# Storing the transposed h and the base by block, and another order of loads, at the border to a recurrence

## The chip, the cores and the metric

The kernel runs on one core of one Trainium2 chip. The metric is the device time of one execution in microseconds; the time before is the median of three runs. The core has a matrix engine (PE, with its weight loads PEld), a vector engine (DVE), a scalar engine (ACT), a general engine (POOL) and a sequencer (SP) that issues most DMAs; POOL issues the others from its own queue. Sixteen DMA engines carry them out.

## The reference: four graph layers, of which the third is a recurrence

For 16 graphs (B) of 1024 nodes (N) with 256 features (D), each layer adds to x a graph operation of h = relu(layernorm(x)). Layers 0 and 1 are products of the adjacency with a linear map of h; layer 3 is an aggregation with a two-layer network. Layer 2 goes through the nodes one after the other:

```python
def step(h, i):
    x = jnp.take(h_e, i, axis=1)
    row = jnp.take(norm_adjT, i, axis=1)
    x_par = jnp.einsum('bj,bjd->bd', row, h)
    iou = x @ W_ioux.T + b_ioux + x_par @ W_iouh.T + b_iouh
    r, z = jnp.split(iou, 2, axis=1)
    r, z = (jax.nn.sigmoid(r), jax.nn.sigmoid(z))
    hc = jnp.tanh(x @ W_coux.T + b_coux + x_par * r @ W_couh.T + b_couh)
    h_new = z * x_par + (1.0 - z) * hc
    h = jax.lax.dynamic_update_slice(h, h_new[:, None, :], (0, i, 0))
    return (h, None)
h_out, _ = jax.lax.scan(step, h_e, jnp.arange(n))
```

## The kernel before

Layers 0 and 1 run together in `layers_0_1`, one graph i per iteration and 16 in all. The order of the work on each engine is written out by hand; a list of hooks puts DVE, ACT, POOL and SP work between the large matmuls (L387, L423). The nodes of each graph are split into 8 blocks (NT) of 128 (P).

Layer 2 does 8 blocks (t), and in each block 8 sub-steps (s) of 16 nodes. All 16 graphs go together: a sub-step has 256 columns, 16 graphs by 16 places. Inside a block the nodes are taken in another order, found at run time and different for each graph; the tables `place` and `table` hold it. A sub-step needs: the gates' part from x (class `Gates`: a POOL copy of 16 columns of each graph from the tile `he` into `hs`, L1039, then three gates of four matmuls each, L1048); the sum over earlier nodes outside the block, `bxt` (made by `base_tasks`, L935 and L949, during the block before; for block 0 loaded from `base_d`); the adjacency inside the block (class `Sub`: POOL gathers its rows from `near_d` into `aj`, L1013, and makes `bd` and `ai` from it, L1029 and L1020); and the weights `wh` (L1102).

What layer 2 needs of h and of the adjacency is made ahead, in a `Job` for each graph, while layer 1 runs. Jobs 0 to 12 run in the iterations i = 9 to 15, two per iteration (an even job, `run_a`, after the first sums, and an odd one, `run_b`, after the second). Jobs 13 to 15 (`tail`) stand behind the last iteration, L814 to L842. Of a job, in its order of work:

- `load` (L511 to L516): SP loads the adjacency pieces `ad` (1 MB) and `ab` (0.5 MB), and h;
- `mask`, `scale`: POOL masks `ad` and `ab` (L524, L526) and scales `ad` (L531, L532); DVE makes `to`, the order as a matrix of ones (L521);
- `turn`: PE transposes h (L542), ACT or DVE copies it to `hT` (L545, L547), POOL stores it (L548);
- `first`: eight matmuls (L554) for the base of block 0, scaled by ACT (L556);
- `order`: PE brings `ad` into the new order (L565, L567), ACT and DVE copy the result to `ao` (L572, L574) after POOL has cleared a corner of it (L561), and POOL stores `near_d` and `next_d` (L575, L576);
- `base`: PE turns the base (L582), DVE copies it (L584), POOL stores it in `base_d` (L585).

`hT` and `ao` of a job share one buffer (both have the name "hT" in a pool with one buffer each), so `ao` is written only when the store of `hT` has read it. The tail jobs use other names: hT of job 14 is in `q`, and so is ao of job 15; ao of job 14 is in `hT`, hT of job 15 in `h1`.

The stores of a job are DMAs on POOL's queue, in this form:

```python
heT_d = dram.tile([B, P, DC, N], F32, name="heT_d")
base_d = dram.tile([B, P, DC, P], F32, name="base_d")
nc.gpsimd.dma_start(heT_d[b], hT)
```

`heT_d` is written in 128 rows of 8 KB for a graph. `load_he(t)` (L998) reads the 128 columns of block t for all graphs, in pieces of 512 bytes: two DMAs of 1 MB (one for each half c of the features), or for block 0 six, since the graphs 0 to 13, 14 and 15 are loaded apart. `bxt` of block 0 is loaded from `base_d` in the same way (L1208).

At the border SP issues in this order: ad and ab of job 14; x; h of graph 15 (a store, L831, that waits for ACT); ad and ab of job 15; wx; four loads of biases; he (six); bxt (six); wh; ab and h for the base of block 1, graphs 0 and 1; he of block 1. POOL's order: the stores and products of jobs 13 to 15, hs for s = 0, the gather aj, bd, ai, hs for s = 1. PE's order: the tail jobs, the gates of s = 0, three matmuls that open the accumulators (L1215), two gates of s = 1, then L1102, the first matmul of the recurrence proper.

Of the kernel before, what the change touches and what calls it, by code (L numbers as in the profile page):

```python
# [9 lines left out]
F32 = mybir.dt.float32  # L10
# [6 lines left out]
P = 128  # L17
B, N, D, H = 16, 1024, 256, 1024
NT = N // P
DC = D // P  # L20
# [22 lines left out]
def gnn_stack(ctx: ExitStack, tc: tile.TileContext, a: dict, out: bass.AP):  # L43
    nc = tc.nc
    const = ctx.enter_context(tc.tile_pool(name="const", bufs=1))
    dram = ctx.enter_context(tc.tile_pool(name="dram", bufs=1, space=DRAM))
# [7 lines left out]

    x2_d = dram.tile([B, N, D], F32, name="x2_d")
    he_d = dram.tile([B, N, D], F32, name="he_d")
    heT_d = dram.tile([B, P, DC, N], F32, name="heT_d")
    hn_d = dram.tile([B, N, D], F32, name="hn_d")
    t_d = {name: dram.tile([B, P, 4, 512], F32, name=name + "_d") for name in ("t1", "t2", "t3", "t4")}

# [10 lines left out]
    table = [const.tile([P, G2, NT, NS], mybir.dt.int32, name=f"table{k}") for k in range(2)]  # L71
    place = const.tile([P, NT * B], F32, name="place")
    dinv = const.tile([P, B, NT], F32, name="dinv")

    def rows(ap):
        return ap.rearrange("(t p) d -> p t d", p=P)
# [9 lines left out]
        nc.gpsimd.tensor_tensor(r, t, mhalf.to_broadcast(shape), ALU.pow)  # L86
        return r

    base_d = dram.tile([B, P, DC, P], F32, name="base_d")
    more = [const.tile([1, N // S], mybir.dt.int32, name=f"more{k}") for k in range(2)]  # L90


# [171 lines left out]
    def layers_0_1():  # L264
        with ExitStack() as st:
            ET = mybir.EngineType
            st.enter_context(tc.manual_schedule(engines={ET.PE, ET.DVE, ET.Activation, ET.Pool, ET.SP}))
            wp = st.enter_context(tc.tile_pool(name="w01", bufs=1))
            big = st.enter_context(tc.tile_pool(name="big01", bufs=1))
# [3 lines left out]
            x, q, h1, h2, g, dis, mean, rs_of, ags = {}, {}, {}, {}, {}, {}, {}, {}, {}  # L273
# [218 lines left out]
            class Job:  # L492
# [42 lines left out]
                def turn(self):  # L535
                    b, to = self.b, self.to
                    hT = big.tile([P, DC, N], F32, name=self.names.get("hT", "hT"))
                    for c in range(DC):
                        for t0 in range(0, NT, 4):
                            pt = psum.tile([P, 512], F32, name="pt")  # L540
                            for t in range(4):
                                nc.tensor.transpose(pt[:, t * P : (t + 1) * P], h2[b][:, t0 + t, c * P : (c + 1) * P],  # L542
                                                    to[:, t0 + t])
                            if t0 == 0 or not self.tail:
                                nc.scalar.copy(hT[:, c, t0 * P : (t0 + 4) * P], pt)  # L545
                            else:
                                nc.vector.tensor_copy(hT[:, c, t0 * P : (t0 + 4) * P], pt)  # L547
                    nc.gpsimd.dma_start(heT_d[b], hT)  # L548

                def first(self):  # L550
                    b = self.b
# [26 lines left out]
                def base(self):  # L578
                    b = self.b
                    pt = psum.tile([P, 512], F32, name="pt")  # L580
                    for c in range(DC):
                        nc.tensor.transpose(pt[:, c * P : (c + 1) * P], self.bs[:, c * P : (c + 1) * P], self.to[:, 0])  # L582
                    bo = self.row("bo").rearrange("p (c i) -> p c i", c=DC)
                    nc.vector.tensor_copy(bo, pt[:, :D].rearrange("p (c i) -> p c i", c=DC))  # L584
                    nc.gpsimd.dma_start(base_d[b], bo)  # L585

                def rest(self):
                    self.first()
# [7 lines left out]
            def side(us):  # L596
                while later:
                    later.popleft()()
                left[0] += us * 1.25
                while left[0] > 0:  # L600
                    cost = next(math, None)
                    if cost is None:
                        break
                    left[0] -= cost
                left[0] = min(left[0], 0.0)
# [37 lines left out]
            job14 = Job(14, {"ad": "at7", "ab": "ds", "to": "at0", "hT": "q", "ao": "hT", "bs": "s1", "bo": "s2"})  # L643
            job15 = Job(15, {"hT": "h1", "ao": "q"})

            for i in range(B):
# [162 lines left out]
                if ahead:  # L809
                    left_of, first, second = combos(q[i + 1])  # L810
                    first()
                side(5.0 if run_a else 3.0)
            h2[14] = big.tile([P, NT, D], F32, name="h2", bufs=2)
            normed(h2[14], x[14], m2.shift, m2.rs, all_)  # L814
            nc.sync.dma_start(rows(he_d[14]), h2[14])
# [9 lines left out]
            job14.mask()  # L825
            run_b.order()
            run_b.base()
            job14.scale()
            h2[15] = big.tile([P, NT, D], F32, name="h2", bufs=2)
            normed(h2[15], x[15], shift, m2.rs, all_)  # L830
            nc.sync.dma_start(rows(he_d[15]), h2[15])  # L831
            job15.load()
            job14.first()
            job14.turn()
            job14.base()
# [3 lines left out]
            job15.base()  # L839
            job15.scale()  # L840
            job14.order()
            job15.order()  # L842
            for _ in math:
                while later:
                    later.popleft()()
# [13 lines left out]
    def layer_2(shared, early):  # L859
        with ExitStack() as st:  # L860
# [5 lines left out]
            def load_w(t, io, co):  # L866
                nc.sync.dma_start(t[:, :, : 2 * D], a[io].rearrange("(c p) e -> p c e", p=P))
                nc.sync.dma_start(t[:, :, 2 * D :], a[co].rearrange("(c p) e -> p c e", p=P))
            load_w(wx, "W_iouxT", "W_couxT")

            bias = wp.tile([P, 3, DC], F32, name="bias")
            bias2 = wp.tile([P, 3, DC], F32, name="bias2")
            with nc.allow_non_contiguous_dma(reason="biases, once"):
                for t, io, co in ((bias, "b_ioux", "b_coux"), (bias2, "b_iouh", "b_couh")):
                    nc.sync.dma_start(t[:, :2].rearrange("p q c -> p (q c)"), a[io].rearrange("(k p) -> p k", p=P))
                    nc.sync.dma_start(t[:, 2], a[co].rearrange("(c p) -> p c", p=P))
            nc.vector.tensor_add(bias, bias, bias2)

            own = wp.tile([P, GB], F32, name="own")
            nc.vector.tensor_reduce(own, ident.rearrange("p (b j) -> p b j", b=GB), AX.X, ALU.add)  # L880
# [14 lines left out]
            def base_tasks(t, bxt):  # L895
# [4 lines left out]
                def load(b):  # L900
                    ab = big.tile([P, NT, P], F32, name="ab")
                    nc.sync.dma_start(ab, a["columns"][b, t])
                    hb = shared.tile([P, NT, D], F32, name="hb")
                    if t > 2:
                        nc.sync.dma_start(hb[:, : t - 2], rows(hn_d[b])[:, : t - 2])
                    if t > 1:
                        nc.sync.dma_start(hb[:, t - 2], hs_d[t - 2][b // GB][b % GB * P : (b % GB + 1) * P])
                    nc.sync.dma_start(hb[:, t:], rows(he_d[b])[:, t:])
                    loaded[b] = ab, hb
# [15 lines left out]
                def task(b, k, held):  # L925
                    def run():
                        if k == 0:
                            if b == 0:
                                mask(0)
                            if b + 1 < B:  # L930
                                load(b + 1)
                            held.append(psum.tile([P, D], F32, name="pf", bufs=3))
                        pb = held[0]
                        ab, hb = loaded[b]
                        nc.tensor.matmul(pb, ab[:, jts[k]], hb[:, jts[k]], start=k == 0, stop=k == len(jts) - 1)  # L935
                        if k == len(jts) - 3 and b + 1 < B:
                            mask(b + 1)
                        if k == len(jts) - 1:
                            del loaded[b]
                            return lambda: summed(b, pb)  # L940
                    return 0.43, run
# [9 lines left out]
                    return 0.44, run  # L951

                load(0)
                tasks = deque()
                for b in range(B):
                    held = []
# [36 lines left out]

            def load_he(t):
                he = big.tile([P, DC, B, P], F32, name="he")
                for b0, b1 in parts if t == 0 else ((0, B),):
                    for c in range(DC):
                        nc.sync.dma_start(he[:, c, b0:b1], heT_d[b0:b1, :, c, t * P : (t + 1) * P].rearrange("b p i -> p b i"))  # L998
                return he

            def row(k, g, t, s):
# [197 lines left out]
                evict()  # L1199

            with tc.manual_schedule(engines={mybir.EngineType.PE, mybir.EngineType.DVE, mybir.EngineType.Activation, mybir.EngineType.Pool}):
                he = load_he(0)
                gx = Gates(he, 0)
                sub = Sub(0, 0)
                bxt = shared.tile([P, DC, B, P], F32, name="bxt")
                for b0, b1 in parts:
                    for c in range(DC):
                        nc.sync.dma_start(bxt[:, c, b0:b1], base_d[b0:b1, :, c].rearrange("b p i -> p b i"))  # L1208
                load_w(wh, "W_iouhT", "W_couhT")
                for task in gx.tasks:  # L1210
                    task()()
                sub.behind()
# [3 lines left out]
                gx.seed_r()  # L1216
                gx.seed_zc()

                near = gx_ahead = None
                behind = []  # L1220
                for t in range(NT):
                    if t == NT - 1:
                        eye = next(early)
                    base_todo = deque()
                    if t + 1 < NT:
                        bxt_next = shared.tile([P, DC, B, P], F32, name="bxt")
                        base_todo = base_tasks(t + 1, bxt_next)
                    n_more = [nc.values_load_multi_w_load_instructions(
# [569 lines left out]
```

## Time and profile before

| | us |
|---|---|
| median of three runs (4225.37 to 4234.3) | 4227.49 |
| the profiled execution | 4226.12 |
| its span, first to last instruction | 4224.4 |
| layer 1 with jobs: 690 to 1297, PE busy | 560.12 of 607 |
| border: 1297 to 1384, PE busy | 58.05 of 87 |
| recurrence after its first sub-step: 1384 to 2960, PE busy | 1525.94 of 1576 |

Times in the profile count from the first instruction. A line of the timeline gives start, duration, engine, line of the kernel, operation, out<-in, shapes and count; in brackets stands how long the engine was idle before, and what ended the wait. POOL's DMA lines are issues: the transfer itself goes on afterwards. SP's issues are marked SPq; where the queue is full, an issue lasts longer. PEclk is the granted share of PE's full clock.

DMA lines of the page:

```profile
DMA  7576657988768454645464554421633434334320
...
q1 hardware_dynamic: 370976, 613.49, 42.5%
q0 software_dynamic: 26080, 109.21, 9.0%
```

q1 is SP's queue, q0 POOL's; the columns are packets, MB and the share of the sixteen engines' time.

### The profile page before, as it was taken

The numbers are of one execution on the slowest core, as the hardware profiler recorded it, in microseconds if no ns is written. First come the engines' busy times: TensorE is split into PE (matmuls) and PEld (weight loads), VectorE is DVE, ScalarE is ACT, GpSimd is POOL, SyncE is SP. The second block draws the span as 40 slices with busy tenths as digits, with TensorE's granted clock in tenths as the row PEclk, the third lists the DMA queues.
The fourth block names the chain that finished last, engine by engine and source line by source line (L and its number), as shares of the span: only waits on it lengthen the run. The fifth ranks groups of instructions, "written<-read, shape, count | busy, mean of one in ns | idle before, by whom it ended". The sixth has DMA issues, their size and how long they took to land. (4 is left out here: it accounts for less than half of the span.)

```text
span 4224.4 us, 56649 instructions
## 1 busy us (share of the span) xinstructions
PE 4018.3 (95%) x19307; PEld 2802.1 (66%) x19307; DVE 2614.6 (62%) x6218; ACT 1635.4 (39%) x4172; POOL 1646.5 (39%) x1740
## 2 busy tenths in 40 slices
PE   7999999998997999999999999998899999999998
PEld 3545455555555888888888888877365665756656
DVE  7888976577762444444444444453577877777776
ACT  3565565544543232232323232323233334333332
POOL 2232223434334324333333333332546355464552
PEclk9999999999998999999999999998899999999999
DMA  7576657988768454645464554421633434334320
GB/s 244 207 238 232 230 200 261 265 301 285 262 212 269 135 197 135 200 136 186 153 193 145 189 163 162 155 99 36 214 120 137 163 120 146 134 121 174 114 100 21
DMA packets 406704, 744.74 MB, mean 176 GB/s; under 512 B 75168, under 2 KB 325664, under 8 KB 365344
## 3 DMA queue, kind: packets, MB, share of 16 engines
q1 hardware_dynamic: 370976, 613.49, 42.5%
q0 software_dynamic: 26080, 109.21, 9.0%
q10 hardware_dynamic: 9216, 16.78, 1.1%
q8 instruction: 210, 3.44, 0.3%
q14 instruction: 222, 1.82, 0.1%
HBM read 538.85 MB, written 183.76 MB: 171 GB/s over the span
## 5 line engine op out<-in xcount | busy, mean ns | idle before, releaser
L86 POOL TENSOR_TENSOR rs<-rs_v,mhalf 128x8 f32<-128x8 f32 (+1 forms) x65 | 112.3, 1728 | 900.4 <-DVE rs_v L82 469.7
L935 PE MATMUL pf<-hb,ab 128*128 128x256 f32 x1568 | 415.2, 383 | 0.0
L1048 PE MATMUL pf<-hs,wx 128*128 128x256 f32 x1536 | 347.7, 383 | 13.0 <-POOL hs L1039 12.7
L1048 PEld LDWEIGHTS pf<-hs,wx 128*128 128x128 f32 x1536 | 293.5, 192 | 56.2 <-POOL hs L1039 13.8
L1348 POOL DMA_INDIRECT hs_d<-h,table x128 | 129.3, 1010 | 464.6 <-ACT gates L1056 404.3
L1576 POOL TENSOR_TENSOR ss<-ss,sq 128x512 f32<-128x512 f32 x224 | 299.2, 1351 | 23.8 <-ACT sq L1574 17.8
L935 PEld LDWEIGHTS pf<-hb,ab 128*128 128x128 f32 x1568 | 272.1, 191 | 37.3 <-issue 6.7
L1053 DVE TENSOR_TENSOR gates<-pf,bias 128x512 f32<-128x512 f32 x128 | 88.5, 692 | 288.3 <-PE pf L1048 248.4
L423 PE MATMUL pmm<-w,ag 128*128 128x256 f32 x1024 | 234.6, 387 | 20.4 <-DVE x L427 8.8
L1639 PEld LDWEIGHTS po<-w,hh 128*128 128x128 f32 x2048 | 237.9, 193 | 16.6 <-issue 11.0
L1639 PE MATMUL po<-w,hh 128*128 128x128 f32 x2048 | 242.1, 277 | 1.4 <-ACT hh L1622 0.7
L423 PEld LDWEIGHTS pmm<-w,ag 128*128 128x128 f32 x1024 | 196.1, 194 | 61.6 <-DVE x L427 12.6
L1574 ACT ACTIVATE sq<-hh 128x512 f32<-128x512 f32 x224 | 141.6, 632 | 197.7 <-POOL ss L1576 118.7
L1522 PE MATMUL ph<-bxt,hb 128*128 128x512 f32 x440 | 198.9, 598 | 4.1 <-ACT hb L1494 2.6
L1146 ACT ACTIVATE r<-pr 128x128 f32<-128x128 f32 (+2 forms) x256 | 57.9, 278 | 366.4 <-PE pr L1102 306.4
L1084 PE MATMUL pf<-bd,h 128*128 128x384 f32 (+4 forms) x512 | 185.1, 451 | 0.8 <-DVE bxt L1087 0.8
L1087 DVE TENSOR_TENSOR bxt<-bxt,pf 128x384 f32<-128x384 f32 (+4 forms) x256 | 128.0, 501 | 82.3 <-PE pf L1084 79.5
L1572 DVE SCALAR_TENSOR_TENSOR hh<-ph,b,u 128x512 f32<-128x512 f32 x192 | 141.5, 749 | 47.0 <-PE ph L1568 36.9
L1622 ACT ACTIVATE hh<-hh,rw 128x512 f32<-128x512 f32 x256 | 158.9, 711 | 24.1 <-DVE hh L1621 24.1
L345 ACT ACTIVATE pt<-x,m_neg 128x256 f32<-128x256 f32 x240 | 114.5, 477 | 109.0 <-DVE m_neg L340 102.7
L1621 DVE TENSOR_TENSOR hh<-hh,po 128x512 f32<-128x512 f32 x256 | 154.3, 679 | 2.9 <-PE po L1618 2.9
L1494 ACT ACTIVATE hb<-x,shift,rs 128x256 f32<-128x256 f32 x120 | 60.9, 591 | 239.6 <-DVE shift L1492 239.6
(371 smaller groups left out, 9283.3 us busy)
## 6 DMA issues: line engine op xcount, KB each, us to landing
at<-in_quarters SPq DMA_DIRECT2D x94, 1024.0 KB
t_d<-at SPq DMA_DIRECT2D x64, 1024.0 KB
ab<-in_columns SPq DMA_DIRECT2D x127, 512.0 KB
bxt<-t_d SPq DMA_DIRECT2D x42, 1024.0 KB
bxt<-in_quarters SPq DMA_DIRECT2D x34, 1024.0 KB
at<-at POOLq DMA_DIRECT2D x30, 1024.0 KB, 7.1
at<-t_d SPq DMA_DIRECT2D x22, 1024.0 KB
pc<-in_own ACTq DMA_DIRECT2D x64, 256.0 KB
```

What stands on the lines that cost most here:

```text
L423: nc.tensor.matmul(po[:, t - t0], ag[:, c, t * P : (t + 1) * P], w[:, c], start=c == 0, stop=c == DC - 1)
L935: nc.tensor.matmul(pb, ab[:, jts[k]], hb[:, jts[k]], start=k == 0, stop=k == len(jts) - 1)
L1048: nc.tensor.matmul(pg[:, e], wx[:, c, q * D + e * P : q * D + (e + 1) * P], self.hs[:, c], start=c == 0, stop=c == DC - 1)
L1084: nc.tensor.matmul(pf, h[:, g, c * P : (c + 1) * P], bd[:, g, b0 : b0 + n, S : S + far], start=True, stop=True)
L1348: nc.gpsimd.indirect_dma_start(out=hs_d[t][g][:, :], out_offset=row(1, g, t, s), in_=h[:, g], in_offset=None)
L1522: nc.tensor.matmul(pa, st[left][:, k], at[q % 6][:, k], start=onto is None and k == 0, stop=k == 3, skip_group_check=True)
L1572: behind3[:] = [nc.vector.scalar_tensor_tensor(hh[q][:, k], ph, b1[:, k : k + 1], u, op0=ALU.add, op1=ALU.add)]
L1574: nc.scalar.activation(sq, hh[q][:, k], AF.Square)
L1576: nc.gpsimd.tensor_tensor(ss[q], ss[q], sq, ALU.add)
L1621: nc.vector.tensor_mul(hh[q][:, k], hh[q][:, k], pr)
L1622: nc.scalar.activation(hh[q][:, k], hh[q][:, k], AF.Silu, scale=rw[:, k : k + 1])
L1639: nc.tensor.matmul(po[:, n], left[:, c, n * P : (n + 1) * P], right[:, c], start=onto is None and n == 0 and c == 0, stop=c == HH - 1, ski ...
```

## The change

1. `heT_d` and `base_d` get another layout: the partition first, then block, half, graph, place. `heT_d[:, t]` is then one run of 16 KB in each partition, and one DMA loads he of a block.
2. A job stores hT in three DMAs: the columns of block 0 at once, the other seven blocks in one DMA for each half (`keep_hT`). Jobs 0 to 12 do all three in `turn`; the tail jobs do the last two after `order` (job 13: after its base).
3. he and bxt of block 0 are loaded in three DMAs each, in turn (graphs 0 to 13, 14, 15).
4. The biases move from the border to the end of iteration 3, their sum to iteration 5, and their tiles to another pool.
5. Job 15's load stands ahead of the store of h of graph 15 on SP; wh is loaded directly behind wx.
6. The gates' inputs for s = 1 are copied directly behind those for s = 0, ahead of the gather aj; the tasks for the base of block 1, with their first two loads, are made ahead of the gates' matmuls.

The order of the instructions on PE and ACT is the same as before; on DVE only the sum of the biases moves.

```diff
-    heT_d = dram.tile([B, P, DC, N], F32, name="heT_d")
+    heT_d = dram.tile([P, NT, DC, B, P], F32, name="heT_d")
+    bias, bias2 = (const.tile([P, 3, DC], F32, name=name) for name in ("bias", "bias2"))
-    base_d = dram.tile([B, P, DC, P], F32, name="base_d")
+    base_d = dram.tile([P, DC, B, P], F32, name="base_d")
...
-                    nc.gpsimd.dma_start(heT_d[b], hT)
+                    nc.gpsimd.dma_start(heT_d[:, 0, :, b], hT[:, :, :P])
+                    self.hT = hT
+                    if not self.tail:
+                        self.keep_hT()
+
+                def keep_hT(self):
+                    for c in range(DC):
+                        nc.gpsimd.dma_start(heT_d[:, 1:, c, self.b], self.hT[:, c, P:].rearrange("p (t i) -> p t i", i=P))
...
-                    nc.gpsimd.dma_start(base_d[b], bo)
+                    nc.gpsimd.dma_start(base_d[:, :, b], bo)
...
+                if i == 3:
+                    with nc.allow_non_contiguous_dma(reason="biases, once"):
+                        for to, io, co in ((bias, "b_ioux", "b_coux"), (bias2, "b_iouh", "b_couh")):
+                            nc.sync.dma_start(to[:, :2].rearrange("p q c -> p (q c)"), a[io].rearrange("(k p) -> p k", p=P))
+                            nc.sync.dma_start(to[:, 2], a[co].rearrange("(c p) -> p c", p=P))
+                if i == 5:
+                    nc.vector.tensor_add(bias, bias, bias2)
...
             run_b.base()
+            run_b.keep_hT()
             job14.scale()
+            job15.load()
             h2[15] = big.tile([P, NT, D], F32, name="h2", bufs=2)
             normed(h2[15], x[15], shift, m2.rs, all_)
             nc.sync.dma_start(rows(he_d[15]), h2[15])
-            job15.load()
...
             job14.order()
+            job14.keep_hT()
             job15.order()
+            job15.keep_hT()
...
             load_w(wx, "W_iouxT", "W_couxT")
-            bias = wp.tile([P, 3, DC], F32, name="bias")
-            bias2 = wp.tile([P, 3, DC], F32, name="bias2")
...
-            nc.vector.tensor_add(bias, bias, bias2)
+            load_w(wh, "W_iouhT", "W_couhT")
...
-                            if b + 1 < B:
+                            if 0 < b < B - 1:
                                 load(b + 1)
...
                 load(0)
+                load(1)
...
                 he = big.tile([P, DC, B, P], F32, name="he")
-                for b0, b1 in parts if t == 0 else ((0, B),):
-                    for c in range(DC):
-                        nc.sync.dma_start(he[:, c, b0:b1], heT_d[b0:b1, :, c, t * P : (t + 1) * P].rearrange("b p i -> p b i"))
+                nc.sync.dma_start(he, heT_d[:, t])
...
-                he = load_he(0)
-                gx = Gates(he, 0)
+                he = big.tile([P, DC, B, P], F32, name="he")
+                bxt, bxt_next = (shared.tile([P, DC, B, P], F32, name="bxt") for _ in range(2))
+                for b0, b1 in parts:
+                    nc.sync.dma_start(he[:, :, b0:b1], heT_d[:, 0, :, b0:b1])
+                    nc.sync.dma_start(bxt[:, :, b0:b1], base_d[:, :, b0:b1])
+                gx, gx_ahead = Gates(he, 0), Gates(he, 1)
                 sub = Sub(0, 0)
-                bxt = shared.tile([P, DC, B, P], F32, name="bxt")
-                for b0, b1 in parts:
-                    for c in range(DC):
-                        nc.sync.dma_start(bxt[:, c, b0:b1], base_d[b0:b1, :, c].rearrange("b p i -> p b i"))
-                load_w(wh, "W_iouhT", "W_couhT")
+                base_todo = base_tasks(1, bxt_next)
...
-                near = gx_ahead = None
+                near = None
```

More of the change, by code (lines that the diff above doesn't have):

```diff
@@ L869, in layer_2 @@
             load_w(wx, "W_iouxT", "W_couxT")
-            bias = wp.tile([P, 3, DC], F32, name="bias")
-            bias2 = wp.tile([P, 3, DC], F32, name="bias2")
[L873 to L876, printed above, removed]
-            nc.vector.tensor_add(bias, bias, bias2)
+            load_w(wh, "W_iouhT", "W_couhT")
             own = wp.tile([P, GB], F32, name="own")
@@ L1223, in layer_2 @@
                         eye = next(early)
-                    base_todo = deque()
-                    if t + 1 < NT:
+                    if t + 1 == NT:
+                        base_todo = deque()
+                    elif t:
                         bxt_next = shared.tile([P, DC, B, P], F32, name="bxt")
```

## The prediction

> **What bounds the kernel now.** I read the page's 40 slices first, then the timeline of one job of layer 1, then the timeline of the border by engine, then the busy times and the granted clock by stretch. From the page:
>
> ```profile
> span 4224.4 us, 56649 instructions
> ...
> PE 4018.3 (95%) x19307; PEld 2802.1 (66%) x19307; DVE 2614.6 (62%) x6218; ACT 1635.4 (39%) x4172; POOL 1646.5 (39%) x1740
> ...
> PE   7999999998997999999999999998899999999998
> ```
>
> PE sets the pace nearly everywhere; a microsecond that PE waits is a microsecond of span, and other engines have room. The edits touch two places: the jobs of layer 1 (slices 7 to 13, 690 to 1297 us) and the border to the recurrence (1297 to 1384). The one dent in the PE row, slice 13, is the border. A job's timeline, job 11:
>
> ```profile
> 1204.08 0.64 POOL L548 DMA_DIRECT2D heT_d<-hT  x1
> 1204.70 0.94 POOL L302 DMA_DIRECT2D at<-at  x1
> ...
> 1208.51 0.11 POOL L561 MEMSET hT<- 128x16 f32 x1 [1.57 <-DMA heT_d<-hT]
> 1208.56 0.59 ACT L572 COPY hT<-pt 128x512 f32<-128x512 f32 x1 [1.11 <-DMA heT_d<-hT]
> ...
> 1209.20 0.33 PE L565 MATMUL pt<-to,ad 128*128 128x128 f32 x1 [1.04 <-ACT hT L572]
> ```
>
> The transposed adjacency goes into the buffer that hT has just left (one buffer, two uses). So the copy at L572 waits until the store of L548 has been read, and PE waits 1.04 us behind the copy: this store already ends too late. The border:
>
> ```profile
> 1324.61 0.29 POOL L526 TENSOR_SCALAR_AFFINE_SELECT ab<-ab 128x128 f32<-128x128 f32 x1 [2.57 <-DMA ab<-in_columns]
> ...
> 1338.29 0.13 POOL L561 MEMSET q<- 128x16 f32 x1
> ...
> 1351.03 1.09 POOL L1013 DMA_INDIRECT aj<-near_d,table  x1 [8.43 <-DMA next_d<-q]
> ...
> 1361.74 0.74 POOL L1039 COPY hs<-he 128x256 f32<-128x256 f32 x2
> 1362.19 5.31 PE L1048 MATMUL pf<-hs,wx 128*128 128x256 f32 x16 [8.92 <-POOL hs L1039]
> ...
> 1367.34 1.89 PE L1102 MATMUL pr<-x,wh 128*128 128x256 f32 x8
> ```
>
> The recurrence's first matmul (L1102) comes at 1367.3, behind the second gates' input, which POOL copies only after the gather aj and its products. By stretch (length, busy us by engine, clock, DMA share, GB/s):
>
> ```profile
> 1342.00:1349.00 7.00, 6.77 (x17) 5.47 (x18) 0.84 (x3) 0.84 (x2) 0.59 (x2) 0.54 1.08 327
> ...
> 1354.00:1362.00 8.00, 0.00 (x0) 0.00 (x0) 0.50 (x2) 0.00 (x0) 4.77 (x5) 0.79 1.09 349
> ```
>
> The DMA engines are full here (share 1.08), and PE, which has had pauses, was granted 0.54 of its clock: the first 12 gate matmuls take 8.5 us (1342.2 to 1350.7) where 12 at 0.43 would take 5.2.
>
> **The change, part by part.**
>
> *Store of hT in three pieces (all 16 jobs).* One DMA of 1024 KB in 8 KB rows becomes one of 128 KB and two of 448 KB, all in rows of 512 bytes: 2048 rows. The trace has no such store. The nearest rows are near_d, next_d and base_d of the same job, on the same queue one after the other: 1024 + 896 + 128 = 2048 rows, 1096 KB. By the packet records their data takes 5.0 us from first byte to last (mean of jobs 0 to 12; 4.2 to 7.9). The present store begins 1.2 us after its issue, so the new one should be read by 1.2 + 5.0 + 0.4 (last byte to semaphore, as now) = **6.6 us** after the first issue, against 4.3 now: +2.3. Lower bound: 256 packets of 4096 bytes at 184 ns over 16 engines are 2.9 us, and the third piece, issued 1.6 us after the first, needs 1.6 to begin (near_d in the odd jobs) and 1.3 to move: 4.9 us. Upper bound: near_d of the even jobs begins only 5.0 to 5.6 us after its issue: 9.6 us and more.
>
> What waits: the copies of L572/L574 and PE behind them. Odd jobs (1, 3, 5, 7, 9, 11): the first copy starts 6.1, 6.2, 4.4, 4.4, 5.0 and 4.5 us after the store's issue, in five of them at the very moment the store lands; each of these moves by +2.3, job 9 by 6.6 - 5.0 = 1.6: 13.1 us. Even jobs (0 to 12): the copy comes 6.5 to 7.7 us after the issue in jobs 0, 4, 6, 8, 10, so almost nothing (0.2); job 2, which waits already, +2.3; job 12 lands at 6.1 now, needed at 6.5: +1.9. Together 17.5 us of PE waiting. PE is busy for 560 of the 607 us of this stretch; some of its other waits are for DVE, which runs work of its own. I let a tenth vanish there: **+15.7**. With 4.9 us it is +4, with 9.6 us +54.
>
> One rule of the Trainium skill bears on this. The packet records have 512-byte packets of the present he load at 28 ns and 8192-byte packets at 309, so 18 against 26 GB/s for one engine. "DMA: Bandwidth & Descriptors", section Specifications, puts the least transfer for line rate at 512 bytes; by it the pieces would move as fast as the 8 KB rows, and this term would fall to about its lower bound, an estimated +4 us. The measured packets decide against it. The same page, section Latency and other measured facts, speaks against the change from another side: row pitches that are large powers of two cost rate, 207 GB/s at 512 KiB and 103 at 4 MiB. heT_d's new pitch is 128 KiB; at the 4 MiB rate the store's 1 MB would need an estimated 10 us. No row of this trace writes so.
>
> *More on POOL's queue.* Two issues more per job, 0.95 us each as near_d's row. Behind them lie rs (L86), the accumulating at<-at, then near_d. The product that needs at<-at comes 8 us after it lands; rs is wanted in the next products. POOL is 40% busy: nothing. In SP's queue the four bias loads (0.57 + 3.60 + 0.67 + 3.50 us there now) move to 312 us, ahead of an x load issued at 311.9 and wanted by ACT at 324.7 (L337): 0, at worst 2. The bias addition is 0.2 us on DVE: 0.
>
> *Border.* Job 15's ad and ab go ahead of a store that waits for ACT until 1310.2; their buffers are free at 1306.7 (last transpose of job 13). ab is then there before 1318, and first (L554) of job 15 follows its turn at 1319.6 instead of 1324.95: -5.4. base_d and near_d of job 14 move from 1331.9 and 1336.4 to 1326.5 and 1331. **Then a new wait:** job 15's order writes into q, which job 14's two late pieces still read. They are queued behind near_d and next_d (whose last byte comes 8.4 us after near_d's issue now). Add 1.7 to 5 us for 896 KB: q is free at 1339.5 to 1344.5, where it is 1338.3 now. Behind the memset of q stand near_d(15), next_d, job 15's two pieces (3.9 us of issues) and the gates' inputs. These would be copied at 1346.5 to 1351.5, 4 to 9 us later than now.
>
> What comes back: both pairs of hs copies now stand ahead of the gather. So PE does 12 gate matmuls (8.5 us at the clock seen there), three seeds (2.6) and 8 gate matmuls (3.5) on end and reaches L1102 at 1361 to 1366, or 3 us sooner at full clock, against 1367.3: **-5** (from -9.5 to +4.5, if the pieces land as late as the 11.5 us that base_d's slowest row shows). The gather may come later without harm: its product bd is needed only at L1355 (1384). The built order also shows the first ab load of the next block waiting for stores that read q; its product comes 20 us later, so it costs nothing unless these land after 1360.
>
> *One load in place of 12, and of 2 per block.* SP's queue falls from 10.7 + 12.3 us to a few; in the recurrence from 2.1 to 0.4 us for each block. PE is 98% busy there (196.6 of 200 us at 1920 to 2120) and never waits for he: 0. wh loaded earlier: needed at L1102, long there: 0.
>
> **Sum.** +15.7 - 5 = +10.7 us. The profiled execution took 4226.1 (span 4224.4): 4236.8; the median of the runs is 1.4 above it: **4238**.
>
> **Rivals.**
> *The stores ride free* (not slower). The pieces land within 5.0 us, as the packet times allow; the odd jobs lose 0.7 each, +4, and the border's gain stays: -1 at -5, and -5.5 at -9.5, so about 4223. For it: heT begins 1.2 us after issue in most jobs. Against it: the triple never took under 4.2 us. It decides from a landing about 5.5 us after the first issue.
> *The scattered write is slow.* Every row of a piece lies a multiple of 16 KB from the next, so the writes crowd; landing at 9.6 us and later gives +54 - 5, about 4276. Against it: the he loads read 512-byte pieces at pitches of 8 KB without delay.
> *The border gives nothing.* q comes free near 1350 because the full DMA holds the pieces up: +15.7 + 4.5, about 4247.
>
> **How the numbers follow.** Forecast 0.47, free stores 0.30, slow write 0.12, no border gain 0.11. A measurement here can tell about 0.2% (8.5 us) from no change. The forecast's own spread (4228 to 4245) lies two thirds over that bound, one third within. Of the free stores half are within, half faster. Slower: 0.31 + 0.12 + 0.11 = 0.54; within: 0.16 + 0.15 = 0.31; faster 0.15. The range 4219 to 4264 takes in free stores with the border's best and most of the slow write.
>
> **What would show it.** Right: in odd jobs the idle time before L572's copy, put down to heT_d, grows by about 2 us, and PE's wait behind it; the stretch 690 to 1297 is longer by 10 to 20 us; at the border the memset of q waits several us for heT_d; no wait for hs is left before the second gates, and L1102 comes about 5 us sooner after the end of layer 1 (1297). Wrong: copies at L572 without a longer wait (the stores are as quick as before), or a wait above 4 us in every job (slow write), or a border shorter by 15 us, which would mean that the full DMA, not the order on POOL, held it.

## The result and the profile after

The changed kernel takes 4246.24 us (median of five runs, 4242.39 to 4248.4) against 4227.49: ratio 1.0039, interval 1.0028 to 1.0051. It is slower by 16 to 19 us; 4238 was forecast. The profiled execution took 4246.59 us. From its page:

```profile
span 4244.9 us, 56723 instructions
...
PE 4031.8 (95%) x19307; PEld 2809.1 (66%) x19307; DVE 2624.5 (62%) x6218; ACT 1634.9 (39%) x4172; POOL 1684.5 (40%) x1772
...
PE   7999999998987999999999999998899999999998
```

PE executes the same 19307 matmuls, but is busy 13.5 us longer: some of them ran at a lower clock, most of them in the jobs, as the stretch of the jobs shows (before, and the same matmuls after; columns as in the prediction):

```profile
690.00:1297.00 607.00, 560.12 (x2098) 326.65 (x2099) 381.33 (x946) 308.41 (x841) 246.06 (x207) 0.98 0.79 258
```

```profile
691.70:1317.90 626.20, 571.72 (x2098) 334.14 (x2099) 389.05 (x946) 308.16 (x841) 276.40 (x233) 0.95 0.79 250
```

Slice 12 (1167 to 1273 us, jobs 10 and 11) has fallen from 9 to 8; the dent of the border, slice 13, is as deep as before. The lines after are numbered 1 to 12 higher than before: L548 is now L549 (first piece) and L556 (late pieces), L561 is L569, L572 is L580, L565 is L573, L1039 is L1050, L1048 is L1059, L1102 is L1113, L998 is L1009. Job 11 in the timeline:

```profile
1218.15 0.83 POOL L549 DMA_DIRECT2D heT_d<-hT  x1
1218.97 2.00 POOL L556 DMA_DIRECT2D heT_d<-hT  x2
...
1224.68 0.11 POOL L569 MEMSET hT<- 128x16 f32 x1 [1.44 <-issue]
1224.75 0.59 ACT L580 COPY hT<-pt 128x512 f32<-128x512 f32 x1 [3.22 <-DMA heT_d<-hT]
...
1225.39 0.33 PE L573 MATMUL pt<-to,ad 128*128 128x128 f32 x1 [3.15 <-ACT hT L580]
```

The three pieces are read 6.5 us after the first issue (4.4 before), and ACT and PE wait 2.1 us longer. The border, by POOL and PE:

```profile
1356.44 1.97 POOL L556 DMA_DIRECT2D heT_d<-q  x2
1366.59 0.11 POOL L569 MEMSET q<- 128x16 f32 x1 [8.17 <-issue]
1366.66 0.59 ACT L580 COPY q<-pt 128x512 f32<-128x512 f32 x1 [15.14 <-DMA heT_d<-q]
...
1367.30 0.48 PE L573 MATMUL pt<-to,ad 128*128 128x128 f32 x1 [12.07 <-ACT q L580]
...
1374.57 1.50 POOL L1050 COPY hs<-he 128x256 f32<-128x256 f32 x4
1375.02 8.05 PE L1059 MATMUL pf<-hs,wx 128*128 128x256 f32 x24 [5.97 <-POOL hs L1050]
...
1388.94 1.89 PE L1113 MATMUL pr<-x,wh 128*128 128x256 f32 x8
```

Job 14's two late pieces, which read q, are issued at 1356.44 and 1357.4 and have read it only at 1366.5; PE, in the order of job 15, waits 12.07 us for it. Everything behind the memset of q on POOL (near_d and the late pieces of job 15, then the copies of hs) moves with it. Once hs is there, PE runs both pairs of gates on end, as the prediction had it. By stretch:

```profile
1342.00:1357.00 15.00, 10.04 (x45) 7.29 (x44) 2.37 (x4) 2.23 (x4) 7.51 (x8) 0.84 1.01 374
1357.00:1370.00 13.00, 1.76 (x7) 1.36 (x7) 1.55 (x4) 1.17 (x2) 1.52 (x3) 0.50 0.68 235
1370.00:1378.00 8.00, 2.98 (x7) 2.44 (x8) 1.33 (x3) 0.00 (x0) 6.40 (x10) 0.50 0.72 203
```

From 1357 to 1370 PE does 1.76 us of work, at half its clock.

Where the time went is read by setting each matmul of PE beside the same matmul before. The changed kernel is 1.7 us late when the jobs begin (690), 20.9 us late at the end of layer 1 (1297), 21.6 us late at the recurrence's first rounds (1384), and 20.6 us late at the end. So **the jobs cost 19.2 us in this profile, and the border, which was to give 5 back, costs 0.7**. The same two differences are given for each experiment below. Profiles with the same store of hT differ there by 4 us (e1 and e7) to 9 us (the changed kernel and e2), so only the timed ratios decide.

### The profile page after: what moved, and what is told of

The parts are those of the page before. It is cut to its first block, busy times and chain, and to the rows that moved or that the text cites. A ratio compares the mean times of both kernels' runs of the same rounds, so it can differ in the third digit from the quotient of the medians.

```text
span 4244.9 us, 56723 instructions
## 1 busy us (share of the span) xinstructions
PE 4031.8 (95%) x19307; PEld 2809.1 (66%) x19307; DVE 2624.5 (62%) x6218; ACT 1634.9 (39%) x4172; POOL 1684.5 (40%) x1772
## 5 line engine op out<-in xcount | busy, mean ns | idle before, releaser
L1059 PE MATMUL pf<-hs,wx 128*128 128x256 f32 x1536 | 345.7, 381 | 6.6 <-POOL hs L1050 6.0
L1059 PEld LDWEIGHTS pf<-hs,wx 128*128 128x128 f32 x1536 | 292.1, 191 | 49.3 <-POOL hs L1050 6.4
```

The costliest lines, as they stand in the source:

```text
L1059: nc.tensor.matmul(pg[:, e], wx[:, c, q * D + e * P : q * D + (e + 1) * P], self.hs[:, c], start=c == 0, stop=c == DC - 1)
```

## The experiments

The first theory: the three pieces hold the buffers of hT and q too long, and nothing else costs anything. Its rival: the new order of loads, of biases and at the border costs the time. Every run is timed against the kernel before on its own chip; the ratio is this run's time over that one's, with its 95% interval, and the two columns between are in us.

| run | jobs, 690 to 1297 | border, 1297 to 1384 | ratio (95% interval) |
|---|---|---|---|
| changed kernel | +19.2 | +0.7 | 1.0039 (1.0028 to 1.0051) |
| e1 order parts alone | +0.6 | -4.0 | 0.9997 (0.9988 to 1.0006) |
| e2 store alone | +10.0 | -0.2 | 1.0038 (1.0025 to 1.0052) |
| e3 jobs 0 to 12 in place | +1.0 | +0.2 | 1.0001 (0.9992 to 1.0010) |
| e4 x tile for q | +14.7 | -2.6 | 1.0036 (1.0022 to 1.0049) |
| e5 he first | +16.4 | +1.3 | 1.0049 (1.0036 to 1.0063) |
| e6 x tile, he first | +16.3 | -11.6 | 1.0014 (1.0005 to 1.0023) |
| e7 order parts, he first | +4.9 | -11.8 | 0.9976 (0.9966 to 0.9987) |
| e8 in place, he first | +1.0 | -7.9 | 0.9979 (0.9970 to 0.9988) |
| e9 one issue | +13.9 | +0.3 | 1.0043 (1.0028 to 1.0058) |
| e10 gates' input ahead | +1.3 | -9.0 | 0.9978 (0.9969 to 0.9986) |
| e11 order, in place, he first | -0.5 | -8.9 | 0.9990 (0.9979 to 1.0001) |

**e1, the order parts alone.** `heT_d`, its store and its loads go back:

```diff
-    heT_d = dram.tile([P, NT, DC, B, P], F32, name="heT_d")
+    heT_d = dram.tile([B, P, DC, N], F32, name="heT_d")
...
-                    nc.gpsimd.dma_start(heT_d[:, 0, :, b], hT[:, :, :P])
+                    nc.gpsimd.dma_start(heT_d[b], hT)
```

> The changed kernel with the old store: heT_d and its loads as before (one store of 1024 KB in 8 KB rows in each job's turn, strided loads of he), everything else as changed (base_d, biases, weights, loads of job 15, gates' input copied ahead). Theory (the three pieces hold hT's buffer too long, and at the border q's): the jobs lose nothing against before (stretch 690 to 1297 within 3 us), the memset of q waits for no late piece, first(15) keeps its -5.5 us and the second gates find hs ready; the first matmul of the recurrence comes 8 to 16 us sooner than before, total 4212 to 4221 us. Rival (the reordered loads, biases, border or the new base_d cost the time): 4235 us or more.

Measured 4222.65 us (before 4223.98), 2 us over the span expected. The jobs lose nothing, so the rival falls for the jobs. But the gain at the border is 4 us in the profile and not 8 to 16, although the memset of q waits for nothing. The timeline shows why; the first line is SP's issue of the last he pieces (graph 15), the second the copy of hs:

```profile
1337.41 1.19 SPq L1214 DMA_DIRECT2D he<-heT_d  x2
...
1349.70 1.43 POOL L1047 COPY hs<-he 128x256 f32<-128x256 f32 x4 [9.38 <-DMA he<-heT_d]
```

Those 128 KB land 12 us after their issue: the change has put 1.8 MB of bxt (graphs 0 to 13) ahead of them on SP's queue, and wh ahead of all of he. The kernel before issued all of he first and copied hs at 1341.8. That was the start of a second theory, tested by e4 to e7.

**e2, the store alone.** The kernel before with the three pieces, all issued in `turn`, and he in one DMA per block:

```diff
-                    nc.gpsimd.dma_start(heT_d[b], hT)
+                    nc.gpsimd.dma_start(heT_d[:, 0, :, b], hT[:, :, :P])
+                    for c in range(DC):
+                        nc.gpsimd.dma_start(heT_d[:, 1:, c, b], hT[:, c, P:].rearrange("p (t i) -> p t i", i=P))
```

> The kernel before with the new heT_d alone: three pieces of 512-byte rows, issued in turn by every job, and he loaded in one DMA per block. Theory: jobs 0 to 12 lose what they lose in the changed kernel, 13 to 20 us, and the border loses up to 5 more, as q is read longer and the gates' inputs stand behind the gather: 4241 to 4253 us. Rival (the order costs it): 4225 to 4231 us.

Measured 4239.29 (before 4223.98), 2 us under the span expected, which was set from 4227.49; the ratio is that of the whole change. The store alone accounts for the whole loss, although this profile shows only 10 us of it in the jobs.

**e3, jobs 0 to 12 in place.** The pieces stay; only the wait for their buffer goes:

```diff
-                    ao = big.tile([P, NT, 2 * P], F32, name=self.names.get("ao", "hT"))
-                    nc.gpsimd.memset(ao[:, NT - 1, P : P + S], 0.0)
+                    ao = ad if b < 13 else big.tile([P, NT, 2 * P], F32, name=self.names.get("ao", "hT"))
+                    if ao is not ad:
+                        nc.gpsimd.memset(ao[:, NT - 1, P : P + S], 0.0)
...
+                    if ao is ad:
+                        nc.gpsimd.memset(ao[:, NT - 1, P : P + S], 0.0)
```

> The changed kernel, but jobs 0 to 12 write the transposed adjacency over its own source ad (each pair of tiles is written behind its own transposes) instead of into the buffer that hT leaves. The three pieces of 512-byte rows, their issues and the DMA traffic stay. The next load of ad then waits for near_d and next_d. Theory (the wait for hT's buffer is the loss): no copy of a job waits for heT_d, the stretch 690 to 1297 falls to that of before or up to 8 us below it, the border stays as changed: 4220 to 4230 us. Rival (512-byte rows or POOL's two more issues per job cost the time by themselves, through the DMA engines or POOL's queue): the jobs stay 15 to 20 us longer, 4240 us or more.

Measured 4226.81 (before 4223.98): no difference from before, and 16 us below the changed kernel. The rows, the bytes and the two more issues on POOL cost nothing beyond some 4 us, the interval's half width; **the wait on the shared buffer is the loss of the jobs**. This run also takes away the waits that the kernel before already had; whether that hides a price of the rows is answered by e8 and e11.

**e4, another buffer for q.**

```diff
-                    ao = big.tile([P, NT, 2 * P], F32, name=self.names.get("ao", "hT"))
+                    ao = big.tile([P, NT, 2 * P], F32, name=self.names.get("ao", "hT"), bufs=3 if self.b == 15 else None)
...
-            job15 = Job(15, {"hT": "h1", "ao": "q"})
+            job15 = Job(15, {"hT": "h1", "ao": "x"})
```

> The changed kernel, but job 15's transposed adjacency goes to a free buffer of the x tiles instead of q, which job 14's two late pieces still read. Theory (the wait on q took the border's gain): the 12 us wait of PE in the order of job 15 goes, the first matmul of the recurrence comes 8 to 14 us sooner, 4232 to 4239 us. Rival (the full DMA queues and PE's low clock hold the border whatever the buffer; near_d of job 15 lands as late as before): 4243 to 4248 us.

Measured 4240.65, between the two spans expected: 1.0036 against 1.0039, nothing gained that the intervals would show. PE's 12 us wait on q does go (near_d of job 15 is issued at 1355.9, not 1370.5). Yet hs is copied at 1370.6, and now he holds it:

```profile
1343.03 0.65 SPq L1217 DMA_DIRECT2D bxt<-base_d  x1
...
1349.23 0.37 SPq L1216 DMA_DIRECT2D he<-heT_d  x1
...
1370.59 1.43 POOL L1050 COPY hs<-he 128x256 f32<-128x256 f32 x4 [10.54 <-DMA he<-heT_d]
```

21 us from the issue of he's last 128 KB to its landing, with 1.8 MB of bxt ahead of it on the queue and the DMA engines at a share of 1.0. The second theory, then: two locks stand one behind the other, q, and he behind bxt (no run parts bxt from wh), and either alone hides the other.

**e5, he first,** with q still waited for (the changed kernel with SP's order of before at this place):

```diff
-            load_w(wh, "W_iouhT", "W_couhT")
...
                     nc.sync.dma_start(he[:, :, b0:b1], heT_d[:, 0, :, b0:b1])
+                for b0, b1 in parts:
                     nc.sync.dma_start(bxt[:, :, b0:b1], base_d[:, :, b0:b1])
+                load_w(wh, "W_iouhT", "W_couhT")
```

> The changed kernel, but SP issues all three pieces of the first he ahead of those of bxt, and wh last, as the kernel before does; the wait on q stays. Theory now: two things hold the gates at the border, each hidden behind the other, q (PE's order of job 15 runs to about 1371) and the last piece of he, which lands behind bxt and wh (in the run with job 15's adjacency in an x tile it landed 21 us after its issue). Taking away the second alone gives little: 4243 to 4248 us. Rival (the loads' order is the whole loss of the border): 4233 to 4239 us.

Measured 4247.01, ratio 1.0049: no gain, as the two locks demand; the memset of q comes at 1364.5.

**e6, both at once** (the edits of e4 and e5).

> Both changes at once: job 15's adjacency in an x tile, and all of he ahead of bxt and wh. Theory of two locks: hs is copied as soon as POOL has issued its stores, 8 to 11 us sooner than with the x tile alone; the first matmul of the recurrence comes as much sooner, total 4228 to 4234 us against 4240.65 with the x tile alone. Rival (the DMA engines are full at the border and only the sum of bytes counts): 4238 us or more.

Measured 4231.24, ratio 1.0014: 9 us less than e4 (1.0036), although the edit that makes the difference, alone, gave nothing in e5. The last 128 KB of he, now ahead of bxt, land 4.2 us after their issue, and hs is copied right behind POOL's own issues, without a wait:

```profile
1357.95 0.30 POOL L892 TENSOR_SCALAR_AFFINE_SELECT before<-ones 128x128 f32<-128x128 f32 x1
1358.20 1.50 POOL L1048 COPY hs<-he 128x256 f32<-128x256 f32 x4
```

The rival (full DMA engines, only the sum of bytes counts) falls: the bytes are the same.

**e7, the order parts with he first** (e1 with e5's order of loads).

> The order parts alone (old store of hT), with all of he ahead of bxt and wh. Theory: there hs waited 9.4 us for the last piece of he, issued behind bxt; that goes, and the border gains what the prediction had hoped for in first(15) and the second gates, 10 to 14 us against before: 4209 to 4215 us, faster than before. Rival (bytes alone count, or another wait of the same size stands behind he): 4220 us or more.

Measured 4216.72 (before 4225.83), ratio 0.9976: faster than both kernels, though 2 us over the span expected. This is what the border's part of the change is worth without either lock, some 10 us.

**e8, the new layout without either wait:** every job in place, he first.

> The new layout without either buffer wait: every job writes its transposed adjacency over its source ad, so that neither hT's buffer nor q is waited for, and all of he goes ahead of bxt and wh. Theory: jobs cost what they cost with jobs 0 to 12 in place (0 to +4 us against before), the border loses its 12 us wait on q and the wait for he: 4213 to 4220 us, faster than before. Rival (POOL's queue, with two more issues per job ahead of the copies of hs, or the bytes): 4225 us or more.

Measured 4217.89 (before 4225.83), ratio 0.9979. The layout that cost 16 us is as good as the old one once nothing waits for its store.

**e9, one issue in place of three.** hT is laid out block by block, so that one DMA takes all 2048 rows:

```diff
-                    hT = big.tile([P, DC, N], F32, name=self.names.get("hT", "hT"))
+                    hT = big.tile([P, NT, DC, P], F32, name=self.names.get("hT", "hT"))
...
+                        nc.gpsimd.dma_start(heT_d[:, :, :, b].rearrange("p t c i -> p (t c) i"),
+                                            hT.rearrange("p t c i -> p (t c) i"))
```

> The changed kernel with hT laid out block by block in SBUF, so that a job's store of hT to the new heT_d is one DMA of 2048 rows of 512 bytes (jobs 13 to 15: one piece and the rest in one more). Same rows, same bytes, one issue on POOL's queue in place of three. If the three issues make it late (the third piece was issued 1.8 us after the first, at 0.82, 1.01 and 1.01 us each): the store is read about 5 us after its issue, the odd jobs lose 0.7 us each in place of 2.3, the stretch 690 to 1297 is 2 to 7 us longer than before, total 4229 to 4236 us. If the rows make it late (2048 packets of 28 ns on 16 engines in place of 128 rows of 8 KB at 309 ns, and the issue grows with its rows): landing 6 us or later, jobs 12 to 18 us longer, 4240 to 4248 us.

Measured 4243.65 (before 4224.68), ratio 1.0043. The view of the store's line:

```profile
L553 POOL DMA_DIRECT2D heT_d<-hT x13: 1156/1182/1208, 696.2 to 1273.7; - x13
...
  ACT hT L582: 16.2, 7
...
DMA to landing us min/median/max: 6.0/6.2/9.5
```

6.2 us with one issue, 6.5 with three, 4.4 with the old rows: the rows make it late, not the issues. ACT still waits 16.2 us in all for this store (7.3 before, 17.8 in the changed kernel).

**e10, the gates' input ahead, alone.** The kernel before with two lines changed:

```diff
-                gx = Gates(he, 0)
+                gx, gx_ahead = Gates(he, 0), Gates(he, 1)
...
-                near = gx_ahead = None
+                near = None
```

> The kernel before with one edit: the second gates' input is copied right behind the first (before the gather aj), nothing else moves, he stays ahead of bxt. It prices that part of the border alone. Theory: PE then does its 24 first and second gate matmuls and the seeds on end from 1342 and reaches the recurrence 5 to 9 us sooner than 1367.3: 4216 to 4222 us. Rival (wh, which is issued at 1348, or the gather's product bd bounds the first rounds): within 2 us of before, 4224 to 4228.

Measured 4216.08 (before 4224.68), ratio 0.9978: at the lower end of the span expected, faster, and level with e7. PE runs the gates of both sub-steps and the seeds nearly on end:

```profile
1350.02 1.50 POOL L1039 COPY hs<-he 128x256 f32<-128x256 f32 x4
...
1350.48 7.13 PE L1048 MATMUL pf<-hs,wx 128*128 128x256 f32 x24 [3.82 <-POOL hs L1039]
...
1360.02 3.62 PE L1048 MATMUL pf<-hs,wx 128*128 128x256 f32 x16
...
1363.47 1.89 PE L1102 MATMUL pr<-x,wh 128*128 128x256 f32 x8
```

(This execution was 5.8 us late at 1297 already.) So these two lines are nearly all that the change's order parts are worth; the earlier load of job 15 adds nothing that the ratios of e7 (0.9976) and e10 (0.9978) would show.

**e11, the old store in place, he first.**

> The order parts with the old store of hT, all of he ahead of bxt and wh, and every job's transposed adjacency written over its source ad. If the waits for hT's buffer that the kernel before already had (1 us in most odd jobs) are worth taking away: 4207 to 4214 us, below 4216.72 of the same without writing in place. Rival (the next load of ad, held up by near_d and next_d, gives that back): 4215 to 4220 us.

Measured 4219.44 (before 4224.68; runs spread from 4210 to 4228), ratio 0.9990: not better than e7, its interval just touches no change. The waits that the kernel before already had are not worth this; as the rival had it, the next load of ad, which then waits for near_d and next_d, may give the gain back, but no run parts that from the spread. e8 differs from this run in the store of hT and its loads alone (both write in place and load he first), and its ratio is not worse, 0.9979 against 0.9990: with no wait on it, the store in rows of 512 bytes costs nothing that can be told.

## Why the prediction was right, and which steps were off

*Store of hT, +15.7.* The landing came as worked out (6.6 us forecast, 6.4 to 6.6 in eleven of thirteen jobs). Five profiles of this code in the jobs (the changed kernel, e2, e4, e5, e6) show 10.0, 14.7, 16.3, 16.4 and 19.2 us, 15.3 in the mean. But the prediction counted all of it as waiting, and that the sum holds is luck: in the changed kernel's profile PE's waits grew by 7.6 us and the same matmuls took 11.6 us longer (over the five profiles 6.4 and 8.9 in the mean). First, in jobs 2, 3 and 12 the old store lands late already (9.0, 6.1 and 5.9 us after its issue, the new one after 10.3, 6.6 and 6.4); the first copy moves by 1.3, 0.5 and 0.5 us, and PE loses 0.5 us or less in each, where 2.3, 2.3 and 1.9 were forecast. The prediction added 2.3 to a delay that doesn't add. Second, in jobs 5, 7, 9 and 11 the copy moves by 2.1 to 2.2 us, near the forecast, but PE is 2.8, 4.0, 4.4 and 6.9 us later by the next job's store; in job 1 the copy moves by 0.6 and PE loses 2.6. Job 7 shows the rest; before:

```profile
1021.17 0.33 PE L565 MATMUL pt<-to,ad 128*128 128x128 f32 x1 [0.87 <-ACT hT L572]
...
1022.78 3.60 PE L387 MATMUL px<-at,q 128*128 128x512 f32 x8
```

and after, with the granted clock of the stretch (third figure from the end) below it:

```profile
1030.03 0.48 PE L573 MATMUL pt<-to,ad 128*128 128x128 f32 x1 [3.08 <-ACT hT L580]
...
1032.30 5.23 PE L388 MATMUL px<-at,q 128*128 128x512 f32 x8
```

```profile
1030.90:1033.90 3.00, 2.96 (x9) 1.64 (x8) 1.82 (x4) 2.72 (x6) 0.67 (x1) 0.50 0.98 176
```

The wait grew from 0.87 to 3.08 us, and behind it PE was granted half its clock: the eight large matmuls take 5.23 us in place of 3.60, the seven transposes 1.75 in place of 0.98. A wait that grew by 2.2 us cost 4.5 by the end of these matmuls. By the trace's clock records PE has half its clock at the waits of jobs 1, 5, 7, 9 and 11 for 3.41, 3.41, 6.83, 3.41 and 13.65 us (before, only 3.41 us in job 11); over the whole stretch of the jobs these times add up to 58.0 us against 20.5. In e3, where the wait is gone, they are 27.3, and the loss is gone with them. The Trainium skill, "TensorE: Matmul & The Clock Gate", Part 1, puts this at an idle window of about 3.4 us, after which the clock is halved until PE has been busy for about as long; here the stretches at half clock are indeed 3.41 us and multiples of it, but less waiting than that was enough: 3.08 us in job 7 and 1.30 in job 1, while 1.54 in job 3 and 0.87 were not. So no length of a wait tells it alone. The prediction read the lower clock at the border and did not apply it to the jobs.

*The two rules it weighed.* "DMA: Bandwidth & Descriptors", Specifications (512 bytes suffice for line rate): by it the store would have been read at about the old time; it took 6.2 us even as one issue. The packets decided rightly against it: 18 GB/s for one engine was read from the loads, and 4096 bytes at 226 ns, as the store's packets have it, are 18 GB/s too. The same page's figures on row pitches of large powers of two begin at 512 KiB; the prediction's 10 us was an estimate by the rate at 4 MiB, and at this pitch of 128 KiB nothing of the sort shows.

*POOL's and SP's queues, 0.* Right for POOL (e3, e8). For SP wrong in one place: **"One load in place of 12 ... 0" and "wh loaded earlier: 0"**. The prediction asked whether wh, he and bxt come in time for their own users, and not what they stand ahead of: bxt and wh now stand ahead of he's last piece. That is worth 9 us (e4 against e6), hidden in the changed kernel by the wait on q.

*Border, -5.* It came out at +0.7, inside the range stated for it (-9.5 to +4.5), and no single step accounts for the difference. The times in the list are those of the changed kernel less 20.9 us, its lateness at the end of layer 1, so that they stand beside the prediction's.

- *Not in the sum, 2.3 us.* The turn of job 15 is 2.3 us late: DVE needs 2.64 us in place of 1.22 to make `to`, and ACT's copy waits for job 13's next_d. first(15) then follows directly, as forecast, and wins 5.5 us against its turn, but it starts at 1321.8 and not at 1319.6, 3.2 us sooner than before and not 5.4.
- *The wait on q, right in kind, 12.1 us long.* "Add 1.7 to 5 us for 896 KB: q is free at 1339.5 to 1344.5" is 8.5 to 13.5 us behind near_d of job 14 (its own terms, 8.4 and 1.7 to 5, make it 10.1 to 13.4). Measured are 12.1 us from that issue to the memset of q: inside that range. The late pieces were issued at the end of a stretch in which the DMA engines were full (share 1.01, 374 GB/s from 1342 to 1357) and landed 8.6 and 9.1 us after their issue. But near_d itself came at 1333.6 and not at 1331, so q is free at 1345.7, past the range.
- *From q to hs, 8.0 us for 7.* PE did the order of job 15 at half its clock; hs is copied at 1353.7, forecast 1346.5 to 1351.5.
- *The gates on end, right.* 13.9 us from the first gate matmul to L1102 (14.6 forecast), which comes at 1368.0 (1367.3 before, 1361 to 1366 forecast).

So the gain of first(15) and that of the second gates (-9 alone, in e10) were both there, and the 12 us on q ate them. The rival "The border gives nothing" has the total within 1 us (4247), but with +4.5 for the border; the changed kernel's profile has +0.7 there and 19.2 in the jobs.

*Free stores, slow write.* Both fell: landing 6.5 us, not below 5.5 and not 9.6.

## What to carry to other kernels

A store that reads a buffer with a second use is priced by its landing, not by its bytes or by the queue that issues it; if another place for the second use costs nothing (here the source tile itself, in e3 and e8), use that before changing a layout. A wait of PE that grows by 1 to 2 us may have to be charged with matmuls at half clock behind it, which doubled its price here. A load that is put earlier in a queue is also to be asked what it is now ahead of; and where two waits end close together, taking one away shows nothing, so take away both (e5 gave nothing, e4 gave nothing, e6 gave 9 us against e4).

## What the runs showed of the hardware

The 2048 rows of 512 bytes stand in the trace's packet records as 256 packets of 4096 bytes at 226 ns (median), where the old store was 128 packets of 8192 bytes at 309 to 333 ns; that is 3.6 against 2.5 to 2.7 us for sixteen engines. The issue of 2048 rows in one DMA took 1.18 us on POOL (0.64 for 128 rows), the first packet followed 1.8 us after the start of the issue (1.2 for the old store). Together this is nearly all of the 1.8 us by which the one-issue store lands later.

Of SP's queue: 128 KB issued behind 1.8 MB landed 12 us (e1, DMA share 0.96) and 21 us (e4, share 1.0) after the issue; issued ahead of it, 4.2 us (e6).

Of PE's clock: in the stretch of the jobs the times at half clock come as 3.41 us and multiples, 20.5 us in all before, 58.0 in the changed kernel, 20.5 to 27.3 in the runs with the old store or in place, and 37.5 to 58.0 in all runs in which the copies wait for the new store.
